# The start of a scan kernel: first rows by products of permuted rows, another layout in DRAM, scaling on other engines

## The chip, the cores and the metric

The kernel runs on one core of a Trainium2 chip, in one launch. Its time is device microseconds of that core; before the change the median of three runs is 4168.44 us (4168.14 to 4168.61).

## The reference, cut to what matters

Two layers follow each other on `x` of 32 images x 48 channels x 64 rows x 128 columns, float32. Each layer normalises (16 groups of 3 channels), then runs four scans, and adds the result to its input:

```python
def step(w, b):
    def f(carry, inp):
        nxt = inp + _conv1d(carry, w, b)      # 5 taps, 48 -> 48 channels
        return (nxt, nxt)
    return f
# rows downwards, rows upwards (same weights), columns to the right, columns to the left
x = x + _L0_conv_ref(_gn(x), ...)
x = x + _L1_conv_ref(_gn(x), ...)
```

In a scan step every row (or column) needs the one before it. Each layer has 63 + 63 row steps and 127 + 127 column steps.

## The kernel before, in words

**Tiling.** Images are taken in four groups of 8 (`GB`). The 128 partitions of a scan tile hold channels of 8 neighbouring positions of a line: 8 x 48 = 384 rows of channels make three tiles of 128 (`NG`), and ten `PIECES` say which channels of which position `e` (0 to 7) stand in which partitions of which tile. The free dimension holds 16 blocks x 8 images = 128 columns. One step (`step`, L889) is nine TensorE products of 128 columns, and three additions on DVE (`scalar_tensor_tensor`, L898), each of which adds bias and the next input row. In the profile one float32 product is two records.

**Order.** `PHASES` lists 12 phases: row scans for each group of images, column scans for each pair of groups, for each layer. `scans` gives the steps of a phase. Everything else stands in an agenda (`at(t, fn, ...)`), where t counts steps, and is issued when that step has been reached. `in_order` keeps every engine's instructions in the order in which they were written, so a waiting instruction holds all that stands behind it on its engine, and on SP's queue every transfer behind it. DMA completion is followed by eight semaphores that SP's and ACT's transfers take in turn: a transfer waits until the one eight places before it has landed.

**What has to happen before the first scan.** `x` in DRAM is ordered by image, channel, row and column; the scan wants its pieces. For the first group this is done in `first_group`, in two ways:

- All rows: `parts` are the images of the group in natural order, 128 partitions with 24 image rows each, 16 transfers of 768 KB. DVE takes their statistics (`InputStats.take`, L507, and `aggregate`, L510). `permute` (L659) turns one image row of all partitions into scan order with four copies of 128x256, on POOL or ACT. `put_out` writes it to the DRAM tensor `xin0`, 512 KB, on SP's queue; 24 such writes in all, in the order `order`, by `put_rows`. `move_rows` reads rows of the scan back from `xin0` in ten transfers (one for each piece) with runs of 128 bytes. Rows 8 to 11 need the first 16 writes, rows 12 to 15 all 24.
- Rows 0 to 7, in addition: `top` holds them with the channel as the partition (rows 0 to 3 in partitions 0 to 47, rows 4 to 7 in 64 to 111). `rows_by_product` (L1281) moves them into scan order by TensorE products with one-hot matrices (`selects`, from `shift`): ten products of 512 columns with 48 rows for each of the two sets, and a copy of each tile out of PSUM on ACT (L1288).

**Weights.** `place_kernel` (L1248) builds the first weight tile in the same way: 38 products of 6 to 390 columns with 48 rows, then copies on ACT (L1251, L1252).

**Scaling.** `scaling` makes scale and offset for each channel and image out of the statistics: products on PE (L385, L396), small operations on DVE, a square root on ACT (L428). Rows 0 to 3 are scaled by `scale_first` (15 instructions on DVE, L745, 9 on ACT, L747), rows 4 to 47 by `scale_rows` on ACT (L722, 24 instructions for each block of rows), rows 48 to 63 by `scale_at_once` on POOL (L733, one multiplication and one addition for a whole block, with scale and offset broadcast).

**Order on the engines.** PE: `place_kernel`, the products of the first set and one tile of the second, the products of `scaling`, two tiles of the second set, steps. SP: weights, `top`, `parts`, 18 writes, loads of rows 8 to 11, 6 writes, loads of rows 12 to 15, then of eight rows at a time. ACT: row copies of the products between permutes, the square root, scaling of rows 0 to 3, permutes, scaling of rows 4 on.

**Later uses of `xin0`.** In the first column phase `load_residual` reads the input of each image group again as columns (`x_by_col`, runs of 8 KB), 12 tiles of 1 MB for each group, to be added to the result (`add_residual`, L824).

Of the kernel before, what the change touches and what calls it, by code (L numbers as in the profile page):

```python
# [29 lines left out]
F32 = mybir.dt.float32  # L30
# [3 lines left out]
C = 48  # L34
# [85 lines left out]
def kernel(  # L120
# [62 lines left out]
    mask_in = wt["left"].rearrange("p i n -> p (i n)")[:, 5 * FULL : 5 * FULL + NG * C]  # L183
# [4 lines left out]
    def kept(name):  # L188
# [8 lines left out]
            dram.tile([E8 * NQ, C, UNIT], F32, tag=f"xin{g}", name=f"xin{g}")  # L197
            for g in range(NGRP)
# [36 lines left out]
    def x_by_col(t, e, j):  # L235


        return t[e * NQ + j]

# [421 lines left out]
    def put_out(g, r, perm):  # L661


        n = perm.shape[-1] // (W * GB)
        for i in range(n):
            at = slice(i * W * GB, (i + 1) * W * GB)
            dma(
                x_put(source[0][g], r + i),
                perm[:, at].rearrange("p (q n) -> p q n", q=NQ),
            )  # L670
# [8 lines left out]
    def move_rows(k, h0, h1, to_dram, q=None):  # L679
# [4 lines left out]
        for h in range(h0, h1, E8):  # L684
            end = min(h1, h + E8)
            for o in range(NG):
                for e, c0, c1, p0 in pieces(o):
                    here = view[p0 : p0 + c1 - c0, o, h % HALF : h % HALF + end - h]
                    if to_dram:
                        there = by_row(t, e, h, end, q)[c0:c1]  # L690
                    else:
                        there = x_by_row(t, e, h, end)[c0:c1]
# [21 lines left out]
    def scale_rows(k, h0, h1):  # L714
# [4 lines left out]
        for o in range(NG):  # L719
# [6 lines left out]
    def scale_at_once(k, h0, h1, eng):  # L726

        _, layer, g = PHASES[k]
        view = row_views(k)[h0 // HALF][:, :, h0 % HALF : h0 % HALF + h1 - h0]
        view = view.rearrange("p o h (k b) -> p o (h k) b", b=GB)  # L730
        for t, op in zip(coeffs[layer, g], (ALU.mult, ALU.add)):
            t = t.unsqueeze(2).to_broadcast([FULL, NG, (h1 - h0) * NK, GB])
            eng.tensor_tensor(view, view, t, op)  # L733

    def scale_first(k, h1, split):

        _, layer, g = PHASES[k]
        scale, offset = coeffs[layer, g]
        view = row_views(k)[0][:, :, 0:h1].rearrange("p o h (k b) -> p o b h k", b=GB)
        for b in range(GB):  # L740
            for o in range(NG):
                it = view[:, o, b]
                by, on = scale[:, o, b : b + 1], offset[:, o, b : b + 1]
                if b < split:
                    nc.vector.tensor_scalar(it, it, by, on, ALU.mult, ALU.add)  # L745
                else:
                    nc.scalar.activation(it, it, AF.Identity, bias=on, scale=by)  # L747
# [62 lines left out]
    def load_residual(k, j, i, nat):  # L810
# [6 lines left out]
        else:  # L817
            for e, c0, c1, p0 in pieces(o):
                dma(nat[p0 : p0 + c1 - c0], x_by_col(t, e, j)[c0:c1])
# [363 lines left out]
    def first_group():  # L1183
# [6 lines left out]
        whole = shift[:, 0 : 2 * FULL + start - C // 3 + ODD]  # L1190
        part = shift[:, whole.shape[-1] : whole.shape[-1] + FULL + ODD]
        SETS = ((0, C), (ODD, ODD + C))

        def selects(piece, s=0):
            e, c0, c1, o, p0 = piece
            t, at = (part, 0) if c0 and p0 else (whole, start - p0 + c0)
            p, q = SETS[s]
            return t[p:q, at + p : at + p + FULL]
# [3 lines left out]
        top = stage[:, 0:2].rearrange("p i n -> p (i n)").rearrange("p (b m) -> p b m", b=GB)  # L1202
        parts = [wide_nat(SLOT + i * SLOT, rows) for i in range(2)]
        stats = InputStats("x0", GB)
        n = W * GB

        kernel = slot[slots(0)[0]][0:C, 0 : TAPS * C + 6]
        zeros = slot[slots(0)[0]][0:C, 512 : 512 + NG * FULL + 6]

        def load_kernel():  # L1210
            nc.vector.memset(zeros, 0.0)
            for j in range(TAPS):
                d, si = divmod(TAPS - 1 - j, 2)
                to = kernel[:, j * C : (j + 1) * C]
                dma(to, w[SIDES[si], 0, DOWN, d, SIDES[0]], nc.scalar if j % 2 else nc.sync)
            aside(kernel[:, TAPS * C :], bias[0:C].rearrange("c l k -> c (l k)"))

        def make_ident():
            nc.vector.memset(shift[:, 0 : whole.shape[-1] + FULL + ODD], 0.0)
            for t, base in ((whole, start), (part, 2 * C - C // 3)):  # L1220
                nc.gpsimd.affine_select(
                    t,
                    t,
                    pattern=[[1, t.shape[-1]]],
                    compare_op=ALU.not_equal,
                    fill=1.0,
                    base=-base,
                    channel_multiplier=-1,
                )
            nc.gpsimd.memset(part[:, 0 : 2 * C], 0.0)  # L1230
            nc.gpsimd.memset(part[:, 2 * C - C // 3 + ODD : 2 * C + ODD], 0.0)

        def place_kernel():
            for i in range(NG):
                ps = ps_rows.tile([FULL, BN], F32, tag=f"rows{i}", name=f"rows{i}")
                todo = [(selects(PIECES[0]), zeros, slice(0, NG * FULL + 6))]
                for piece in PIECES:
                    e, c0, c1, o, p0 = piece
                    if o == i:
                        m = selects(piece)  # L1240
                        for run in WEIGHT_RUNS:
                            if run[0:4] == (c0, c1, i, p0):
                                _, _, _, _, at, to, n = run
                                todo.append((m, kernel[:, at : at + n], slice(to, to + n)))
                        tail = slice(NG * FULL, NG * FULL + 6)
                        todo.append((m, kernel[:, TAPS * C :], tail))
                for j, (lhs, rhs, to) in enumerate(todo):
                    nc.tensor.matmul(  # L1248
# [167 lines left out]
```

## Time and profile before

| | |
|---|---|
| median of three runs | 4168.44 us (4168.14 to 4168.61) |
| profiled execution | 4172.8 us, span 4171.0 us |
| mean granted TensorE clock | 0.99 |
| PE busy | 4073.2 us, 98% |
| DVE, ACT, POOL busy | 2135.8, 1287.2, 786.9 us |
| first scan step starts (timeline of PE) | 61.86 us |
| steps without a wait from (timeline of DVE) | 108.02 us |

The page is of one profiled execution. A busy share is an average over the whole span; the stretch that the change touches is the first 110 us or so, that is 2.6% of it, so it has to be read from the timelines of single engines. The granted clock is shown as 1.00 up to its first recorded change; the duration of a TensorE record says more there.

### The profile page before, as it was taken

What the parts mean: (1) busy time and instruction counts of PE and PEld (TensorE: products, weight loads), DVE (VectorE), ACT (ScalarE), POOL (GpSimd) and SP (SyncE); (2) the same over time, 40 slices, a digit from 0 to 9 for tenths busy, and PEclk for the clock granted to TensorE, in tenths of its full rate; (3) what the DMA queues carried; (4) which work ended last, traced back from release to release, by engine and by line L of the source; (5) the groups of instructions that cost most, each with busy time, mean ns of one, the idle gap of its engine ahead of it and who ended that gap; (6) DMA issues with size and microseconds to landing.
All of it is one profiled execution on the core that took longest, in us unless ns stands there. A gap on an engine that the chain in (4) does not pass through costs nothing. (4 is left out here: it accounts for less than half of the span.)

```text
span 4171.0 us, 90280 instructions
## 1 busy us (share of the span) xinstructions
PE 4073.2 (98%) x36724; PEld 4042.8 (97%) x36724; DVE 2135.8 (51%) x6501; ACT 1287.2 (31%) x2525; POOL 786.9 (19%) x737
## 2 busy tenths in 40 slices
PE   8999999999999999999999999999999999999994
PEld 6999989999999999999999999999999999999994
DVE  5454444456654454444447664444444444444444
ACT  6845000526974553000007863423000002200122
POOL 3530010434322010010014220000000005610353
PEclk9999999999999999999999999999999999999997
DMA  9987669669978999258409979959389019999699
GB/s 294 230 181 120 113 126 207 213 147 260 203 192 168 164 172 154 45 96 188 119 13 282 185 142 150 142 87 149 53 143 207 1 53 240 293 263 156 143 235 195
DMA packets 2206496, 680.57 MB, mean 163 GB/s; under 512 B 2008464, under 2 KB 2157184, under 8 KB 2179968
## 3 DMA queue, kind: packets, MB, share of 16 engines
q1 hardware_dynamic: 2062096, 582.09, 68.5%
q10 hardware_dynamic: 141424, 87.19, 8.7%
q8 instruction: 289, 4.73, 0.5%
q0 software_dynamic: 2560, 5.51, 0.5%
q14 instruction: 127, 1.04, 0.1%
HBM read 397.77 MB, written 295.14 MB: 166 GB/s over the span
## 5 line engine op out<-in xcount | busy, mean ns | idle before, releaser
L722 ACT ACTIVATE arena<-arena,offset,scale 128x256 f32<-128x256 f32 (+2 forms) x840 | 581.3, 791 | 346.9 <-DMA arena<-mid 179.9
L824 POOL TENSOR_TENSOR arena<-arena 128x2048 f32<-128x2048 f32 x80 | 362.6, 4547 | 1484.3 <-PE step_10l L889 462.8
L659 POOL COPY arena<-arena 128x256 f32<-128x256 f32 x332 | 196.6, 652 | 454.1 <-DMA arena<-in_x 406.9
L597 ACT ACTIVATE early<-arena 128x256 f32<-128x256 f32 x192 | 129.5, 675 | 446.0 <-POOL arena L824 439.9
L889 PE MATMUL step_00r<-arena,early 128*128 128x128 f32 x2286 | 252.5, 274 | 9.8 <-DMA arena<-arena 6.0
L889 PEld LDWEIGHTS step_00r<-arena,early 128*128 128x128 f32 x2286 | 251.8, 186 | 10.5 <-DVE arena L898 5.3
L889 PE MATMUL step_01r<-arena,early 128*128 128x128 f32 x2286 | 252.2, 274 | 7.0 <-DMA arena<-arena 5.9
L889 PEld LDWEIGHTS step_01r<-arena,early 128*128 128x128 f32 x2286 | 251.5, 186 | 7.6 <-issue 6.3
L889 PE MATMUL step_11r<-arena,early 128*128 128x128 f32 x2286 | 249.3, 272 | 0.0
L889 PE MATMUL step_00l<-arena,wleft 128*128 128x128 f32 x2286 | 249.2, 272 | 0.0
L889 PEld LDWEIGHTS step_11r<-arena,early 128*128 128x128 f32 x2286 | 248.7, 184 | 0.5 <-DVE arena L898 0.3
L889 PEld LDWEIGHTS step_00l<-arena,wleft 128*128 128x128 f32 x2286 | 248.7, 184 | 0.0
L889 PE MATMUL step_10l<-arena,wleft 128*128 128x128 f32 x2286 | 248.5, 272 | 0.0
L889 PE MATMUL step_11l<-arena,wleft 128*128 128x128 f32 x2286 | 248.5, 272 | 0.0
L889 PE MATMUL step_01l<-arena,wleft 128*128 128x128 f32 x2286 | 248.4, 272 | 0.0
L889 PE MATMUL step_10r<-arena,early 128*128 128x128 f32 x2286 | 248.4, 272 | 0.0
L889 PEld LDWEIGHTS step_10l<-arena,wleft 128*128 128x128 f32 x2286 | 248.4, 184 | 0.0
L889 PEld LDWEIGHTS step_11l<-arena,wleft 128*128 128x128 f32 x2286 | 248.4, 184 | 0.0
L889 PEld LDWEIGHTS step_01l<-arena,wleft 128*128 128x128 f32 x2286 | 248.4, 184 | 0.0
L889 PEld LDWEIGHTS step_10r<-arena,early 128*128 128x128 f32 x2286 | 248.4, 184 | 0.0
L282 ACT COPY early<-arena 128x1 f32<-128x1 f32 x2 | 0.4, 191 | 707.2 <-DVE arena L898 707.2
L846 ACT COPY arena<-arena 128x256 f32<-128x256 f32 x172 | 99.6, 657 | 363.0 <-POOL arena L824 272.8
(200 smaller groups left out, 7073.3 us busy)
## 6 DMA issues: line engine op xcount, KB each, us to landing
xin<-arena SPq DMA_DIRECT2D x91, 512.0 KB, 3.9
arena<-in_x SPq DMA_DIRECT2D x18, 2048.0 KB, 12.1
arena<-xin SPq DMA_DIRECT2D x96, 384.0 KB, 10.2
arena<-mid SPq DMA_DIRECT2D x384, 96.0 KB, 3.0
upb<-arena SPq DMA_DIRECT2D x192, 192.0 KB, 3.9
arena<-upb SPq DMA_DIRECT2D x96, 384.0 KB, 12.1
arena<-xin SPq DMA_DIRECT2D x180, 192.0 KB, 4.3
mid<-arena SPq DMA_DIRECT2D x32, 1024.0 KB, 11.2
```

Source lines behind the costliest of these rows:

```text
L282: fn(*args)
L597: nc.scalar.activation(junk[:, 0:n], view[:, b], AF.Identity, accum_out=self.sum[:, i, j : j + 1])
L659: copy(dst[:, r, q], src[:, r0 + r, q])
L722: nc.scalar.activation(args[0], args[0], AF.Identity, bias=args[2], scale=args[1])
L824: eng.tensor_tensor(unit, unit, nat, ALU.add)
L846: copy(by_w(perm)[:, a], src[:, a])
L889: nc.tensor.matmul(part(whole(ps[o])[0:m], -s), weights[:, i, at : at + m], part(src(i), s), start=seen[o] == 1, stop=seen[o] == left[o],)
```

## The change

- Rows 0 to 7: the image rows are loaded first, ahead of the weights, `top` gets 16 more channels in partitions 48 to 63 and 112 to 127, so that all 128 are filled; `permute` turns the four rows of `top` into `turned` (two on POOL, two on ACT), and the products read `turned` in runs of 32 elements. The selection matrices have 128 rows, one set for each half, with zeros in the other half.
- The products of rows 0 to 7 come ahead of `place_kernel`, which is split into its three tiles and stands between permutes; `kernel` and `zeros` are now 128 partitions, in `early`.
- `xin0` is laid out in natural order: channel, row, quarter, and within it 8 positions x 32. `put_out` writes 4 KB in one run for each partition instead of four of 1 KB; `move_rows` still reads runs of 128 bytes; `load_residual` reads runs of 1 KB instead of 8 KB for the first group.
- Rows 0 to 7 are scaled by `scale_at_once` on DVE, two rows at a time, rows 4 to 7 among the first steps. `scale_first` goes. Rows 8 to 39 are shared by `scale_shared`: tile 0 on ACT, tiles 1 and 2 on POOL. Rows 12 to 23 come in blocks of four rows, not in one of four and one of eight. The last permutes alternate between POOL and ACT.

```diff
         [
             dram.tile([E8 * NQ, C, UNIT], F32, tag=f"xin{g}", name=f"xin{g}")
+            if g
+            else dram.tile([C, H, NQ, LINE], F32, tag=f"xin{g}", name=f"xin{g}")
...
+    def natural_row(t, e, h0, h1):
+
+        return t.rearrange("c h q (e n) -> e c (h q) n", e=E8)[e, :, h0 * NQ : h1 * NQ]
+
+    def natural_put(t, r):
+
+        t = t.rearrange("c (a i) q n -> i (c a) (q n)", i=E8)[r % E8]
+        return t.rearrange("(p r) n -> r p n", r=PR // E8)[r // E8]
+
+    def natural_col(t, e, j):
+
+        return t.rearrange("c (a i) q n -> i q c a n", i=E8)[e, j]
 
...
+            one = perm[:, i * W * GB : (i + 1) * W * GB]
+            if g:
+                dma(x_put(source[0][g], r + i), one.rearrange("p (q n) -> p q n", q=NQ))
+            else:
+                dma(natural_put(source[0][g], r + i), one)
...
-                        there = x_by_row(t, e, h, end)[c0:c1]
+                        there = (x_by_row if g else natural_row)(t, e, h, end)[c0:c1]
...
+    def scale_rows(k, h0, h1, groups=range(NG)):
...
-        for o in range(NG):
+        for o in groups:
             for b in range(GB):
...
+    def scale_at_once(k, h0, h1, eng, o0=0):
 
         _, layer, g = PHASES[k]
...
+        view = row_views(k)[h0 // HALF][:, o0:, h0 % HALF : h0 % HALF + h1 - h0]
         view = view.rearrange("p o h (k b) -> p o (h k) b", b=GB)
         for t, op in zip(coeffs[layer, g], (ALU.mult, ALU.add)):
...
+            t = t[:, o0:].unsqueeze(2).to_broadcast([FULL, NG - o0, (h1 - h0) * NK, GB])
             eng.tensor_tensor(view, view, t, op)
-
...
-                dma(nat[p0 : p0 + c1 - c0], x_by_col(t, e, j)[c0:c1])
+                here = nat[p0 : p0 + c1 - c0]
+                if pair or half:
+                    dma(here, x_by_col(t, e, j)[c0:c1])
+                else:
+                    dma(by_line(here), natural_col(t, e, j)[c0:c1])
...
-        whole = shift[:, 0 : 2 * FULL + start - C // 3 + ODD]
-        part = shift[:, whole.shape[-1] : whole.shape[-1] + FULL + ODD]
+        span = 2 * FULL + start - C // 3 - ODD
         SETS = ((0, C), (ODD, ODD + C))
 
         def selects(piece, s=0):
             e, c0, c1, o, p0 = piece
-            t, at = (part, 0) if c0 and p0 else (whole, start - p0 + c0)
-            p, q = SETS[s]
-            return t[p:q, at + p : at + p + FULL]
+            at = s * (span + FULL)
+            at += span if c0 and p0 else start - p0 + c0
+            return shift[:, at : at + FULL]
 
...
+        top = wide_nat(3 * SLOT, four)
+        turned = stage[:, 2:4].rearrange("p i n -> p (i n)").rearrange("p (r n) -> p r n", n=n)
...
+        free = WEIGHTS + 2 * n
+        zeros = early[:, free : free + NG * FULL + 6]
+        free += NG * FULL + 6
+        kernel = early[:, free : free + TAPS * C + 6]
 
...
+                other = slice(ODD, FULL) if p0 == 0 else slice(0, ODD)
+                nc.gpsimd.memset(shift[other, at : at + span + FULL], 0.0)
+                nc.gpsimd.memset(part[:, 0 : 2 * C], 0.0)
...
         def rows_by_product(s, o):
-            src = top[SETS[s][0] : SETS[s][1]]
-            src = src.rearrange("p b (r k e) -> p e r k b", k=NK, e=E8)
             ps = ps_rows.tile([FULL, four * N], F32, tag=f"rows{o}", name=f"rows{o}_{s}")
+            src = turned.rearrange("p r (q e n) -> p e r q n", q=NQ, e=E8)
...
-                    ps.rearrange("p (r k b) -> p r k b", r=four, b=GB),
+                    ps.rearrange("p (r q n) -> p r q n", r=four, q=NQ),
...
+        def scale_shared(h0, h1):
+            scale_rows(0, h0, h1, range(1))
+            scale_at_once(0, h0, h1, pool, 1)
+
+        src = x[0:GB].rearrange("b c h w -> c b (h w)")
+        for s, (p0, p1) in enumerate(SETS):
+            here, queue = src[:, :, s * four * W : (s + 1) * four * W], (nc.sync, nc.scalar)[s]
+            dma(top[p0:p1], here, queue)
+            dma(top[p1 : p0 + ODD], here[0 : ODD - C], queue)
         load_kernel()
-        for s, (p0, p1) in enumerate(SETS):
-            src = x[0:GB].rearrange("b c h w -> c b (h w)")
-            dma(
-                top[p0:p1],
-                src[:, :, s * four * W : (s + 1) * four * W],
-                nc.scalar if s else nc.sync,
-            )
         for i in range(2):
             for b in range(GB):
                 dma(parts[i][:, b], flat(b)[:, i * rows * W : (i + 1) * rows * W])
...
         make_ident()
-        place_kernel()
+        for r in range(four):
+            permute(top, r, turned[:, r], ((pool, act)[r % 2],))
+        for o in range(NG):
+            rows_by_product(0, o)
         make_masks()
         for b in range(GB):
             stats.take(0, parts[0], b)
-        put_rows(pool, act, pool, act)
-        rows_by_product(0, 0)
-        put_rows(pool, act, pool, act)
-        rows_by_product(0, 1)
-        put_rows(pool, act, pool)
-        rows_by_product(0, 2)
-        put_rows(pool)
-        rows_by_product(1, 0)
+        for o in range(NG):
+            put_rows(pool, act)
+            rows_by_product(1, o)
+        for o in range(NG):
+            put_rows(pool, act)
+            place_kernel(o)
         for b in range(GB):
             stats.take(NBN // 2, parts[1], b)
             stats.aggregate(b)
         put_rows(act, pool)
         for _ in scaling("x0", 0, 0, stats, x_masks):
             pass
-        scale_first(0, 4, 5)
+        scale_at_once(0, 0, 2, nc.vector)
+        scale_at_once(0, 2, 4, nc.vector)
         put_rows(pool, act, pool, act)
-        rows_by_product(1, 1)
-        rows_by_product(1, 2)
         move_rows(0, 8, 12, False)
-        put_rows(pool, act, pool, pool, pool, pool)
-        move_rows(0, 12, 16, False)
-        scale_rows(0, 4, 8)
-        scale_rows(0, 8, 12)
-        scale_rows(0, 12, 16)
-        for h in range(16, 64, 8):
-            move_rows(0, h, h + 8, False)
+        put_rows(pool, act, pool, act, pool, act)
+        scale_shared(8, 12)
+        for h in (12, 16, 20, 24, 32, 40, 48, 56):
+            end = h + (four if h < 24 else E8)
+            move_rows(0, h, end, False)
             if h < 40:
-                scale_rows(0, h, h + 8)
+                scale_shared(h, end)
         take_in(1, 0, nats1[0])
 
     in_order(first_group)
+    at(starts[0] + 1, scale_at_once, 0, 4, 6, nc.vector)
+    at(starts[0] + 3, scale_at_once, 0, 6, 8, nc.vector)
     at(starts[0] + 10, scale_rows, 0, 40, 48)
     for j in range(1, 4):
         at(starts[0] + 22 + j, take_in, 1, 4 * j, nats1[j])
```

## The prediction

> **What bounds the kernel now.** I read the page first: TensorE is busy almost all of the span, and ahead of its first full slice there is an 8.
>
> ```profile
> span 4171.0 us, 90280 instructions
> PE 4073.2 (98%) x36724; PEld 4042.8 (97%) x36724; DVE 2135.8 (51%) x6501; ACT 1287.2 (31%) x2525; POOL 786.9 (19%) x737
> PE   8999999999999999999999999999999999999994
> ```
>
> So the scans are bound by TensorE, and this change can only win what the first 110 us lose. The profiled execution took 4172.8 us (span 4171.0, 1.8 outside it), 4.4 above the median 4168.44; I carry the difference found in the trace over to the median.
>
> Next the timeline of PE up to 130 us. Columns: start, duration, what, count (two records for one float32 product), idle before.
>
> ```profile
> 2.63 20.39 PE L1248 MATMUL rows<-arena,wleft 48*128 48x390 f32 x76 [2.63 <-POOL wleft L1221]
> 22.88 20.53 PE L1281 MATMUL rows<-arena,wleft 48*128 48x512 f32 x26
> 48.84 13.09 PE L1281 MATMUL rows<-arena,wleft 48*128 48x512 f32 x14
> 61.86 10.71 PE L889 MATMUL step_00d<-arena,early 128*128 128x128 f32 x74
> 74.60 8.16 PE L889 MATMUL step_00d<-arena,early 128*128 128x128 f32 x72 [2.03 <-DVE arena L898]
> 96.22 9.80 PE L889 MATMUL step_00d<-arena,early 128*128 128x128 f32 x72 [3.98 <-DVE arena L898]
> ```
>
> The first step starts at 61.86, held by the products of rows 0 to 7. Four steps (72 records) take 8.16 us at full rate, hence 0.113 us a record of 128 columns; the first 74 records took 10.71, 2.3 too many. The 512-column records of L1281 take 13.09/14 = 0.93 us; at the steps' rate they would take 0.45. So the preparation runs at half rate throughout, with 48 of 128 rows of the array in use, although PE is never idle in it.
>
> Then DVE's waits among the steps, and who ends them:
>
> ```profile
> 74.19 0.61 DVE L898 SCALAR_TENSOR_TENSOR arena<-step_00d,bd,arena 128x128 f32<-128x128 f32 x2 [2.28 <-ACT arena L722]
> 83.67 0.61 DVE L898 SCALAR_TENSOR_TENSOR arena<-step_00d,bd,arena 128x128 f32<-128x128 f32 x2 [1.48 <-ACT arena L722]
> 95.81 0.61 DVE L898 SCALAR_TENSOR_TENSOR arena<-step_00d,bd,arena 128x128 f32<-128x128 f32 x2 [4.24 <-ACT arena L722]
> 108.02 0.61 DVE L898 SCALAR_TENSOR_TENSOR arena<-step_00d,bd,arena 128x128 f32<-128x128 f32 x2 [2.57 <-DMA arena<-xin]
> ```
>
> These are rows 4, 8, 12 and 16. After 108.02 nothing stops PE until 577 us. So the number to predict is when row 16 can be added. Last, SP's queue and ACT, which deliver it:
>
> ```profile
> 63.73 6.06 SPq L271 DMA_DIRECT2D arena<-xin  x10
> 73.98 2.27 SPq L271 DMA_DIRECT2D xin<-early  x2
> 82.38 67.72 SPq L271 DMA_DIRECT2D arena<-xin  x68
> 64.65 18.93 ACT L722 ACTIVATE arena<-arena,offset,scale 128x64 f32<-128x64 f32 x48
> 86.22 24.27 ACT L722 ACTIVATE arena<-arena,offset,scale 128x64 f32<-128x64 f32 x53 [2.63 <-DMA arena<-xin]
> ```
>
> Rows 12 to 15 need all 24 `put_out` transfers on DRAM, so their loads start at 82.38 whatever PE does. Up to there the DMA engines are full (share 1.02 and 1.08 in the windows 23:43 and 49:61).
>
> **The change, part by part.**
>
> *Clock of the new products.* All products now use 128 rows. 20 products of 512 columns cost 20 x 1.86 = 37 us at half rate, 18 at full; `place_kernel` 20.4 or 10. No row of this trace shows selection products at 128 rows; the nearest are the steps: 128 rows, and after 61.86 they lose 2.3 us, so about 4.6 us at half rate, then full. I take full rate after 4.6 us. The Trainium skill (TensorE: Matmul & The Clock Gate, Part 1) says that about 3.4 us of sustained matmuls lift the clock, and names no number of rows; by it the products of before would have been fast too. The trace disagrees: 40 us of unbroken products stay at half rate. That leaves rows used, or something else in these products, as the reason, and the second is the first rival.
>
> *PE's order.* The image rows must land (about 12), then four `permute` calls, two on POOL and two on ACT, each 4 copies of 0.59: 4.7 us, to 16.5. First set 9 + 2.3 to 28, second set to 37, `place_kernel` to about 47. DVE's statistics (L507, from 12.67 to 44.5, unbroken) shift with the first part by about 1.5, to 46. So the scaling products wait for PE until 47, not 44.7; the scaling took 6.8 us (44.69 to 51.46), so the offsets come at 54.
>
> *Scaling of rows 0 to 7.* 15 + 9 instructions on DVE and ACT (7.4 us) become `scale_at_once` on DVE: 8 operations of 768 elements. L824 on DVE (2048 elements) takes 2.28 alone and 2.73 beside POOL's copies: 1.12 ns an element, so 0.86, plus up to 0.45. Rows 0 and 1: two, 2.6 us. First step at 57, 5 us earlier than 61.86. The last four operations stand among the steps; DVE has 0.7 to 1 us of idle between two steps, so each pair (1.7 to 2.6) delays PE by about 1. The skill's page SBUF — State Buffer speaks against this placing: a DVE operation with two SBUF inputs and a GpSimd one exclude each other. The 2.73 against 2.28 agrees in kind, 0.45 us each; at worst 8 x 0.45 = 3.6 us, but all of it before row 12.
>
> *What is late next.* From 57, steps reach row 4 at 67, row 8 at 75 and row 12 at 83. Row 12 isn't there, so the 5 us are off the path. Rows 12 to 15 come by the DMA stream:
> - The loads start at 0.80 instead of 2.18: -1.4. Two pads of 16 channels add 2 x 256 KB; at the 270 GB/s of the window 2:12 that is +1.9. They stand on both queues ahead of the weights, and semaphore lanes are shared by eight transfers, so `parts` now waits for the image rows to land: +1.2, an estimate between 0 and 3. Sum +1.7.
> - `put_out` writes 4 KB runs instead of four of 1 KB. The window 44:62 (1 KB runs) gives 379 GB/s, 13:37 (6 KB runs) 418, 696:708 (8 KB) 425. 512 KB: 1.38 against 1.25 us, 24 times: -3.1 (0 to -3.5).
> - SP's order is the same: 18 puts, 10 loads, 6 puts, loads. ACT's permutes end about 62 after its wait for the standard deviation at 51; no put waits for them, as the DMA needs put 17 at 64. Loads of rows 12 to 15 start at 82.38 + 1.7 - 3.1 = 81.0.
> - They keep runs of 128 B: 52 rows in 67.72 us, 1.30 a row. Four rows 5.2, landing 2.2: 88.4.
> - `scale_shared`: ACT 8 x 0.39, hidden beside POOL's two operations of 1024 elements. L733 (3072) takes 6.71, so 2 x 2.24 = 4.5. POOL has nothing else. Row 12 at 92.9 instead of 95.81.
> - PE then stood idle 10 us instead of 4. The 9.80 after a wait of 4 lost 1.6, the start 2.3; I take 2.3. Four steps 7.9 + 2.3: row 16 at 103.1. Rows 16 to 19 land at 93.6 and are scaled by 98: no wait. The next blocks are close: rows 24 to 31 land at about 109, two POOL operations of 2048 take 9, 118, and PE asks at 119.
>
> Sum: 103.1 against 108.02, -4.9; 4168.44 - 4.9 = 4163.5. Own range -9 to 0.
>
> *Natural order, later.* Residuals of group 0 (12 units) are read in 1 KB runs instead of 8 KB. In the window 852:878 these 48-partition loads run at 185 GB/s, in 1 KB runs 128-partition writes at 379, so run length isn't what limits them; I take nothing. But from 1000 to 1190 us the DMA share is 1.0, and PE waits 7.7 us for row data at 1193.06. 12 MB at 185 GB/s are 65 us; 10% either way gives or takes 6.5.
>
> **The rivals.**
> 1. *Half rate stays* (slower). If one-hot weights don't lift the clock, PE takes 37 + 20.4 from 16.5, to 74, then 6.8 and 2.6: first step at 83, row 12 not before 108. ACT's row copies and permutes wait between the products, so put 23 and the loads slide to about 98, row 12 to 110, row 16 to 119: +11, 4179.5. Against it: the steps' own rise. It decides from 12 us of delay on, which is how long PE may be late before row 12 asks.
> 2. *Full rate for the products, half for the weights* (products there have 6 to 390 columns). `place_kernel` ends at 57, put 15 is issued 3 us later, row 12 at 96, row 16 at 106: 4166.5.
> 3. *More than the sum*: the stream gains its 3.5, the wait at 1193 shrinks by up to 6.5: down to 4155, about 4158.
> 4. *Loads of natural order are slower*: the wait at 1193 grows by 15 or more: 4178.
>
> **How the numbers follow.** 0.2% is 8.3 us, about what a measurement can tell from no change. My case 0.38 and rival 2 0.12 lie within it: 0.50. Rival 3 0.30: faster. Rival 1 0.14 and rival 4 0.06: slower, 0.20. The range 4155 to 4180 takes in rival 3 and the middle of rivals 1 and 4; the likeliest case alone spans 4159 to 4168.
>
> **What would show it.** Right: 512-column records near 0.45 us after about 21 us; first step near 57; loads of rows 12 to 15 near 81 on SP; a longer idle ahead of row 12 than the 4.24 before, none at row 16. Wrong: records of 0.93 throughout; PE waiting at `place_kernel`'s end; loads of rows 12 before 78 or after 85; another length of the wait near 1190.

## The result, and the profile after

The median is 4177.6 us (12 runs, 4168.49 to 4184.83) against 4168.72 for the kernel before on the same chip: ratio 1.0021, interval 1.0012 to 1.0030. It is slower by 0.2%, about 9 us; 4163.5 was forecast. The profiled execution took 4171.1 us, 6.5 under its median, so it can't be compared by its total with the profile of before (4172.8, 4 above its median). I compare by place instead. First the head of the page:

```profile
span 4169.4 us, 90214 instructions
PE 4050.3 (97%) x36724; PEld 4033.1 (97%) x36724; DVE 2138.5 (51%) x6495; ACT 1251.3 (30%) x2440; POOL 828.6 (20%) x751
PE   5999999999999999999999999999999999999994
```

TensorE is busy 23 us less than before, since its preparation runs at full rate, and yet nothing is won: the first slice shows 5 instead of 8. Now the timeline of PE (start, duration, what, count, idle before; the views end at 130 and at 200 us, so the last two rows go on):

```profile
17.49 19.35 PE L1298 MATMUL rows<-arena,wleft 128*128 128x512 f32 x40 [17.49 <-POOL arena L674]
36.67 10.52 PE L1270 MATMUL rows<-early,wleft 128*128 128x390 f32 x76
59.46 5.57 PE L894 MATMUL step_00d<-arena,early 128*128 128x128 f32 x36 [6.11 <-DVE arena L748]
81.29 6.57 PE L894 MATMUL step_00d<-arena,early 128*128 128x128 f32 x36 [16.27 <-DVE arena L903]
88.03 42.23 PE L894 MATMUL step_00d<-arena,early 128*128 128x128 f32 x382 [0.16 <-DVE arena L903]
177.17 23.00 PE L894 MATMUL step_00d<-arena,early 128*128 128x128 f32 x192 [1.93 <-DVE arena L903]
```

The products and `place_kernel` end at 47.2, as forecast, and the first step starts 2.4 earlier than before. Then come two waits that were not forecast: 16.27 us after step 2, and 1.93 at 175, where the kernel before had none. DVE and POOL show their causes:

```profile
77.00 0.96 DVE L748 TENSOR_TENSOR arena<-arena,scale 128x768 f32<-128x768 f32 x1 [13.57 <-DMA xin<-arena]
78.00 2.98 DVE L748 TENSOR_TENSOR arena<-arena,offset 128x768 f32<-128x768 f32 x1
176.76 0.87 DVE L903 SCALAR_TENSOR_TENSOR arena<-step_00d,bd,arena 128x128 f32<-128x128 f32 x3 [3.11 <-POOL arena L748]
```

```profile
77.05 3.11 POOL L748 TENSOR_TENSOR arena<-arena,scale 128x1024 f32<-128x1024 f32 x1 [11.66 <-DMA xin<-arena]
163.25 6.69 POOL L748 TENSOR_TENSOR arena<-arena,scale 128x3072 f32<-128x3072 f32 x1 [28.28 <-DMA arena<-xin]
170.02 6.71 POOL L748 TENSOR_TENSOR arena<-arena,offset 128x3072 f32<-128x3072 f32 x1
```

The scaling of rows 4 and 5 waits for a `put_out`, though no put touches these rows. Rows 48 to 55 (3072 elements on POOL) are ready at 176.7, and DVE, which adds row 48, has waited 3.11 us. Before the change, the same scaling started 10.6 us earlier:

```profile
152.65 6.69 POOL L733 TENSOR_TENSOR arena<-arena,scale 128x3072 f32<-128x3072 f32 x1 [90.33 <-DMA arena<-xin]
```

The row loads on SP are late, and SP's waits from 120 to 170 us (below the rows of its queue: us in total, times, longest) say for whom:

```profile
12.57 18.03 SPq L286 DMA_DIRECT2D arena<-in_x  x16
66.57 5.59 SPq L286 DMA_DIRECT2D arena<-xin  x10
82.30 81.90 SPq L286 DMA_DIRECT2D arena<-xin  x80
```

```profile
SPq L286 <- POOL arena L748: 8.9, 1, 8.9
```

`parts` is issued from 12.57, not 2.65. Loads of rows 12 on start at 82.30, against 82.38 before, and take 81.90 us. Before, all of these loads had landed by 155.0; now by 167.5. Once, for 8.9 us, SP stands behind POOL.

**A ledger by rows.** As PE has no wait of over 0.35 us between row 51 and 570 us in any run, the moment when DVE adds row 51 sums up the opening. The table gives the start of that addition and of earlier ones, from the DVE timelines; the last column is the median less row 51. (Row 16's first addition starts at 105.10 before and at 111.24 after the change; the 108.02 of the prediction are its second and third.)

| run | row 17 | row 25 | row 51 | median | before, same chip | ratio, interval | rest |
|---|---|---|---|---|---|---|---|
| before | 109.59 | 125.39 | 176.75 | 4168.44 | | | 3991.7 |
| before_again | 109.70 | 125.50 | 176.85 | 4168.27 | 4169.14 | 1.0003 (0.9994 to 1.0012) | 3991.4 |
| after | 113.16 | 128.96 | 184.19 | 4177.60 | 4168.72 | 1.0021 (1.0012 to 1.0030) | 3993.4 |
| after_again | 113.19 | 128.99 | 184.64 | 4178.72 | 4171.57 | 1.0018 (1.0009 to 1.0027) | 3994.1 |
| put_pieces | 107.74 | 126.28 | 185.97 | 4185.98 | 4169.70 | 1.0035 (1.0022 to 1.0048) | 4000.0 |
| put_pieces_again | 107.12 | 125.56 | 184.69 | 4179.53 | 4169.14 | 1.0023 (1.0014 to 1.0033) | 3994.8 |
| pool_by_tile | 111.80 | 127.60 | 178.95 | 4175.85 | 4169.70 | 1.0012 (1.0004 to 1.0021) | 3996.9 |
| rows32_by_tile | 112.64 | 128.44 | 179.79 | 4176.11 | 4167.96 | 1.0018 (1.0010 to 1.0027) | 3996.3 |
| tiles_one_by_one | 107.50 | 123.77 | 175.12 | 4170.64 | 4171.57 | 1.0003 (0.9993 to 1.0013) | 3995.5 |
| old_layout | 111.66 | 127.61 | 186.18 | 4183.00 | 4171.57 | 1.0026 (1.0017 to 1.0035) | 3996.8 |
| before_natural | 108.00 | 125.42 | 176.77 | 4173.48 | 4171.57 | 1.0004 (0.9995 to 1.0012) | 3996.7 |
| tiles_weights_first | 104.80 | 122.36 | 173.72 | 4166.94 | 4169.70 | 0.9992 (0.9983 to 1.0001) | 3993.2 |
| pieces_pool_weights | 106.39 | 122.19 | 173.54 | 4168.60 | 4169.70 | 0.9997 (0.9988 to 1.0006) | 3995.1 |
| rows96_no_pad | 103.48 | 119.46 | 170.81 | 4166.61 | 4167.96 | 0.9994 (0.9986 to 1.0002) | 3995.8 |
| rows96_again | 103.70 | 120.01 | 171.36 | 4166.40 | 4169.14 | 0.9992 (0.9984 to 1.0001) | 3995.0 |
| rows64 (one run) | 116.21 | 132.01 | 185.59 | 4183.68 | 4167.96 | | 3998.1 |

The changed kernel loses 7.4 to 7.9 us by row 51: 3.6 by row 17, the rest at rows 48 to 50. That is as much as the 7 to 9 of the medians.

### The profile page after: what moved, and what is told of

Its sections match the earlier page's. It is cut to its first block, busy times and chain, and to the rows that moved or that the text cites. A ratio compares the mean times of both kernels' runs of the same rounds, so it can differ in the third digit from the quotient of the medians.

```text
span 4169.4 us, 90214 instructions
## 1 busy us (share of the span) xinstructions
PE 4050.3 (97%) x36724; PEld 4033.1 (97%) x36724; DVE 2138.5 (51%) x6495; ACT 1251.3 (30%) x2440; POOL 828.6 (20%) x751
## 5 line engine op out<-in xcount | busy, mean ns | idle before, releaser
L737 ACT ACTIVATE arena<-arena,offset,scale 128x256 f32<-128x256 f32 (+2 forms) x744 | 538.1, 817 | 386.8 <-DMA arena<-mid 147.7
## 6 DMA issues: line engine op xcount, KB each, us to landing
arena<-upb SPq DMA_DIRECT2D x96, 384.0 KB, 12.3
```

The lines of the kernel that those rows point to most:

```text
L737: nc.scalar.activation(args[0], args[0], AF.Identity, bias=args[2], scale=args[1])
```

## The experiments

Theory one: an operation that spans several tiles (rows 4 and 5 of all three, `128x3x256`, one tile 32 rows apart from the next) is made to wait for every transfer that uses the rows in between, and holds later transfers itself. Theory two: the natural order in DRAM makes loads or later residuals slower.

**The changed kernel again.** No edit.

> The changed kernel once more, for a second profile and more times: its first profile (4171.1 us) is near the low end of its 12 runs (4168.5 to 4184.8), so most of the 9 us to the kernel before may lie in waits that the first profile does not show. Both theories: median 4175 to 4180. Theory one (the wait of the spanning DVE operation): the 13.6 us wait of DVE ahead of row 4 is there again, row 16 is added at 111 +- 1. Theory two (natural order in DRAM): row 16 the same, but the later waits of PE (near 175, 584, 1188 and 1857 us), 19.7 us in sum in the first profile against 27.8 before the change, come out larger here, by up to 10 us, if the profiled execution is a slower one.

Row 51 at 184.64, DVE's wait 13.30, median 4178.72: as theory one says, but theory two gave the same for row 16 and the median, so this run does not decide between them. PE's waits of over 0.35 us after 100 us were 24.6 instead of 19.7 us in sum (a wait at 607 us of 3.86 instead of 0.47): the rest of the kernel varies by some us from one execution to the next.

**One operation for each tile.**

```diff
         for t, op in zip(coeffs[layer, g], (ALU.mult, ALU.add)):
-            t = t[:, o0:].unsqueeze(2).to_broadcast([FULL, NG - o0, (h1 - h0) * NK, GB])
-            eng.tensor_tensor(view, view, t, op)
+            for o in range(o0, NG):
+                it = t[:, o].unsqueeze(1).to_broadcast([FULL, (h1 - h0) * NK, GB])
+                eng.tensor_tensor(view[:, o - o0], view[:, o - o0], it, op)
```

> The changed kernel, with scale_at_once as one operation for each of the tiles instead of one across two or three tiles. Theory one (an operation that spans tiles waits for every transfer that uses the rows between): the first operation of rows 4 and 5 starts by 66 with less than 2 us of idle ahead of it, instead of 77.00 after 13.57; row 8 is added near 84 instead of 95.53, row 12 near 96 (its rows are ready on GpSimd at 95), row 16 near 104 instead of 111.24; the median falls by 7 from that of the changed kernel, to about 4170. Theory two (the time is lost by the natural order in DRAM, in the later waits): the trace up to row 16 changes as just said, but the median stays within 3 of the changed kernel's, about 4176.

DVE and PE of this run:

```profile
65.36 1.08 DVE L749 TENSOR_TENSOR arena<-arena,scale 128x256 f32<-128x256 f32 x3
96.52 25.88 PE L895 MATMUL step_00d<-arena,early 128*128 128x128 f32 x216 [4.53 <-DMA arena<-xin]
```

The operations of rows 4 and 5 start at 65.36 without a wait, PE has no wait of over 0.35 us from 96.52 to 570, the last row loads are issued by 157.2, and the median falls by 8.1 to 4170.64 (4178.72 on the same chip). The spanning operations cost what the change lost. Which of them, this run can't say.

**The layout of before in the changed kernel; natural order in the kernel before.** In the first, `xin0`, its puts, row loads and residual loads are as before the change; in the second these four are the only change.

> The changed kernel, with the DRAM tensor of the first group laid out as before the change (each put again four runs of 1 KB, residuals again in runs of 8 KB). Theory one: puts take 1.38 instead of 1.25 us, 24 of them 3.1 us; rows 12 to 15 land 3 us later, row 16 is added near 114; median 4178 to 4181. Theory two: the later waits shrink and lose their spread (before: 9 us in 12 runs, after: 16), median 4170 or below.

> The kernel before, with the natural order in DRAM alone. Theory one: puts 1.25 instead of 1.38 us, loads of rows 12 to 15 start at 79.5 instead of 82.4, row 16 is added near 105 instead of 108; median 4166, 0 to 3 below the kernel before. Theory two: slower than the kernel before by 5 to 9, median 4174 to 4177, with a wider spread and larger waits of PE near 580 and 1190.

SP and ACT of before_natural:

```profile
78.36 73.41 SPq L286 DMA_DIRECT2D arena<-xin  x70
64.89 60.41 ACT L737 ACTIVATE arena<-arena,offset,scale 128x64 f32<-128x64 f32 x135
```

Natural order alone brings the loads of rows 12 to 15 forward by 4.0 us (82.38 to 78.36). Row 16 gains 4.1, and by row 19 all of it is gone: ACT, which does all the scaling there, works without a break from 64.89 to 125.30 and is late next. The median is 1.9 higher, and the interval reaches from 2 below to 5 above: theory two's loss of 5 to 9 is not seen, and neither is theory one's gain of 0 to 3. In old_layout loads of rows 12 start at 86.32, 4.0 later, row 51 comes at 186.18 and the median rises by 4.3 to 4183.00. Theory one said 4178 to 4181, theory two 4170 or below, so theory two falls, and theory one has the direction and too small a size. One thing was not expected by either: old_layout has no wait ahead of rows 4 and 5, although its operation spans the tiles as well, and row 16 comes at 109.74, not near 114.

**The puts described otherwise.** What differs for DVE between the two layouts is how the put is written on the SBUF side, one run of 1024 or four of 256. So this run changes the description alone:

```diff
-                dma(natural_put(source[0][g], r + i), one)
+                there = natural_put(source[0][g], r + i)
+                there = there.rearrange("p (q n) -> p q n", q=NQ)
+                dma(there, one.rearrange("p (q n) -> p q n", q=NQ))
```

> The changed kernel, with one line of put_out: the transfer's two sides are written as four runs of 256 each that follow each other (the same 4 KB for each partition, natural order in DRAM). Instructions, their order and the transfer itself stay; only the waits that the compiler derives differ: the DVE operations of rows 0 to 7 span three tiles as before. Theory one (the 13.6 us wait is a dependence that the compiler sees between the spanning DVE operation and a put of one run, and no data need it): the operation of rows 4 and 5 starts by 65, row 12 is added near 95 (GpSimd is done with its rows at 95.0), row 17 near 107.5 instead of 113.2; GpSimd's spanning operations stay, so row 48 still waits, and rows 48 to 50 lose 2 to 4 as they do in the changed kernel; median 5 to 6 below the changed kernel, near 4173. Rival (rows 4 to 7 wait for data that they need, or for DVE itself): the wait stays over 10 us and the median within 2 of 4178.7.

PE (the view ends at 200 us) and POOL:

```profile
57.37 5.76 PE L896 MATMUL step_00d<-arena,early 128*128 128x128 f32 x36 [4.90 <-ACT arena L674]
124.81 49.08 PE L896 MATMUL step_00d<-arena,early 128*128 128x128 f32 x430 [2.17 <-DVE arena L905]
177.98 22.23 PE L896 MATMUL step_00d<-arena,early 128*128 128x128 f32 x176 [4.08 <-DVE arena L905]
164.06 6.71 POOL L750 TENSOR_TENSOR arena<-arena,scale 128x3072 f32<-128x3072 f32 x1 [28.74 <-DMA arena<-xin]
```

The wait of 13.6 us is gone with instructions, order and bytes unchanged, so it came from the compiler's view of the overlap, not from data. Why it sees an overlap with one run of 1024 and none with four of 256 was not settled. Row 17 comes at 107.74 as expected. But the median did not fall by 5; it rose by 7. All that was won is lost again: row 25 waits for POOL (2.17), row 48 for POOL (4.08; SP again stands 8.9 us behind POOL), since POOL starts rows 48 to 55 at 164.06 whatever PE has won. So the largest gap of PE, 16.27 us, was worth nothing by itself. The Trainium skill (Perfetto Trace Analysis, Optimization Strategy) advises to find the gaps of the contended engine and to start what blocks them sooner; here that, done at the largest gap alone, gave no gain.

> The run with puts in four runs again, as its median (4186.0, of 6 undisturbed runs) lies 7 above the changed kernel's, while its row 51 is only 1.3 later. If the start of the kernel accounts for the time, row 51 is at 186.0 again and the median is 8 to 12 above the kernel before, near 4180. If taking away DVE's wait costs more later on, the median is again 14 or more above it.

The second time: row 51 at 184.69, median 4179.53, 10.4 above the kernel before. The 4186 seems a high draw of what follows row 51 (rest 4000.0, here 3994.8); that taking away DVE's wait gains nothing holds in both.

**GpSimd by tile; its rows 32 to 39 alone by tile.** The loop of tiles_one_by_one, for POOL only (`if eng is nc.gpsimd:`), and for one block of rows only:

```diff
+            if o0 and h0 == HALF:
+                for o in range(o0, NG):
+                    it = t[:, o].unsqueeze(1).to_broadcast([FULL, (h1 - h0) * NK, GB])
+                    eng.tensor_tensor(view[:, o - o0], view[:, o - o0], it, op)
+                continue
```

DVE's operations span as in the changed kernel.

> The changed kernel, with GpSimd's scaling by tile, DVE's as changed. Theory one: DVE's wait of 13.6 us ahead of row 4 stays and row 17 stays at 113.2; SP's wait of 8.9 us for GpSimd at the loads of rows 40 to 47 goes, the last row loads are issued by 157 instead of 164.4, GpSimd begins with rows 48 to 55 near 141 instead of 163.7, and PE doesn't wait at row 48: row 51 is 3.6 behind the kernel before instead of 7.4 to 7.9; median 4 below the changed kernel, 4174 to 4175. Rival (that wait is contention with DVE or late loads, not the spanning): row 48 waits 2 us or more as in the changed kernel.

> The changed kernel, with GpSimd's scaling of rows 32 to 39 alone by tile (two multiplications and two additions of 1024 elements instead of one each of 2048); all other scaling as changed, DVE's spanning operations too. Theory (one spanning operation holds one transfer of rows 40 to 47 on SP's queue, and with it all row loads behind it, which costs the wait at row 48): SP's wait of 8.9 us for GpSimd goes, the last row loads are issued by 156, GpSimd begins with rows 48 to 55 near 154 instead of 163.7, PE doesn't wait at row 48, row 51 is 3.6 behind the kernel before instead of 7.4 to 7.9 (DVE's wait of 13 us stays, row 17 at 113); median near 4175, as by tile on GpSimd altogether (4175.9). Rival (it takes all of GpSimd's operations, or the load rate of the natural order): row 48 still waits 2 us or more, median within 2 of 4178.7.

POOL of rows32_by_tile; then the window of 124 to 136 us, first of the changed kernel, then of rows32_by_tile (PE, PEld, DVE, ACT, POOL busy, clock, DMA share, GB/s):

```profile
122.99 4.68 POOL L750 TENSOR_TENSOR arena<-arena,scale 128x1024 f32<-128x1024 f32 x2
154.93 6.71 POOL L753 TENSOR_TENSOR arena<-arena,scale 128x3072 f32<-128x3072 f32 x1 [22.62 <-DMA arena<-xin]
```

```profile
124.00:136.00 12.00, 12.00 (x111) 12.00 (x111) 5.92 (x19) 4.22 (x8) 9.07 (x2) 1.00 0.33 52
```

```profile
124.00:136.00 12.00, 12.00 (x112) 12.00 (x111) 5.75 (x18) 7.46 (x15) 8.32 (x4) 1.00 0.98 149
```

Splitting one multiplication and one addition in two takes SP's wait away. In the changed kernel the DMA engines moved 52 GB/s in that stretch, because the first load of rows 40 to 47 of tile 1 (issued at 135.00, 9.8 after the one before it) stood behind the scaling of rows 32 to 39 of tiles 1 and 2; between these rows it lies in memory. In this run they moved 149, the loads were issued by 155.1, POOL began 8.3 us earlier and row 48 did not wait. Row 51 is at 179.79, 4.4 to 4.9 earlier, as expected; with all of POOL by tile, 178.95. Their medians, 4176.1 and 4175.9, are 8.2 and 6.2 above the kernel before, more than the 3.0 and 2.2 of row 51. The rest column says the same: these two have 3996 to 3997. In the whole time the ratios, 1.0018 and 1.0012, can't be told from the changed kernel's 1.0021 and 1.0018: what POOL's wait alone costs is shown at row 51, and not at the end.

So with both spans the loss at row 51 is 7.4 to 7.9; without DVE's, 7.9 and 9.2; without POOL's, 2.2 and 3.0; without both, -1.6. Each hides the other in part: at row 51 POOL's alone keeps all of the loss, DVE's alone 2.2 to 3.0. In the whole time only the run without both is clearly lower.

**The start of the stream.** Weights ahead of the image rows, as before the change, with scaling by tile on both engines; then the same with the puts in four runs and DVE's spanning operations.

```diff
+        load_kernel()
         for s, (p0, p1) in enumerate(SETS):
...
             dma(top[p1 : p0 + ODD], here[0 : ODD - C], queue)
-        load_kernel()
```

> Scaling by tile on DVE and GpSimd, and the weights issued ahead of the image rows as before the change. Theory (the stream of puts and loads sets row 12, and the image rows ahead of the weights hold parts back by lanes: parts from 12.57 instead of 2.65): parts are issued from about 3, loads of rows 12 to 15 start 3 to 4 earlier than the 84.0 of the run by tile, row 17 is added near 104 (107.5 by tile), median 3 to 4 below the run by tile, 4167. Rival (the DMA engines are full from 2 us on whichever comes first): the image rows land later, the permutes and products slide, and the loads of rows 12 to 15 start within 1.5 of 84.0; median within 2 of 4170.6.

> Puts described in four runs, DVE's scaling across tiles, GpSimd's by tile, weights ahead of the image rows. Theory: as in the run by tile with weights first, but DVE's first scaling takes 8 operations of 768 instead of 24 of 256, so the first step comes 2 to 3 earlier; this is off the path, and row 17 and the median are the same as there within 2: row 17 near 104, median 4167. If the first step counted, the median would be 2 to 3 lower than in that run.

`parts` is issued from 2.6 us, and loads of rows 12 to 15 start at 82.11, 1.9 earlier than by tile, not 3 to 4. Row 17 comes at 104.80 and row 51 at 173.72, 1.4 earlier than by tile. In the second run row 1 is added 2.7 earlier (61.15 instead of 63.90), row 17 1.6 later (106.39; 104 was expected), and row 51 is the same within 0.2: the first step is off the path.

**96 rows without pads.**

```diff
-        SETS = ((0, C), (ODD, ODD + C))
+        SETS = ((0, C), (C, 2 * C))
+        USED = 2 * C
...
-            return shift[:, at : at + FULL]
+            return shift[0:USED, at : at + FULL]
...
-            dma(top[p1 : p0 + ODD], here[0 : ODD - C], queue)
```

> As the run with puts in four runs, GpSimd by tile and weights first, but the image rows stand in partitions 0 to 47 and 48 to 95, without the two transfers of 16 more channels, and the products and weights use 96 rows of the array. Theory (the pads and the slow image rows, 211 GB/s from 2 to 12 us, hold the stream of puts): loads of rows 12 to 15 start 1.5 to 2.5 earlier than 82.5, at 80 to 81; row 17 at 104 to 105 instead of 106.4; median 2 below that run, near 4166. On the clock: if it goes by rows used, 96 could lie on either side; at half rate the products take 37 us and the weights 20, PE is done with them at 74, and the first step comes near 83, median over 4180; at full rate 512-column records near 0.45 as with 128. I expect full rate.

> The version with 96 rows and no pads again, against the kernel before: row 51 5.9 ahead of it in the trace, median 1.4 below in the first comparison, interval 0.9986 to 1.0002. If the 5.9 us hold to the end, median 4 to 6 below the kernel before; if the rest of the kernel takes more when it starts earlier, 1 to 2 below as before.

SP, first of pieces_pool_weights, then of this run:

```profile
31.97 14.92 SPq L286 DMA_DIRECT2D xin<-arena  x9
82.50 73.75 SPq L286 DMA_DIRECT2D arena<-xin  x80
```

```profile
28.76 14.88 SPq L286 DMA_DIRECT2D xin<-arena  x9
79.35 73.88 SPq L286 DMA_DIRECT2D arena<-xin  x80
```

Without the two pads, 512 KB, the stream is 3.2 us earlier. Row 51 is 5.9 and 5.4 ahead of the kernel before, but the medians are only 1.4 and 2.7 below it, and both intervals hold 1. With tiles_weights_first (2.8 below) these are the lowest versions found; none is a proven gain.

In the two profiles of this version the clock is lifted 5.25 and 4.70 us after the first product. In the second profile it does not hold: `place_kernel` takes 11.79 us instead of 10.53, and the granted clock falls to 0.50 at 45.9, while PE is still busy without a break. First the row of `place_kernel`, then the window that follows the fall, with the clock ahead of the DMA share and the GB/s:

```profile
36.90 11.79 PE L1286 MATMUL rows<-early,wleft 96*128 96x390 f32 x76
45.90:48.70 2.80, 2.80 (x15) 2.80 (x15) 0.00 (x0) 0.51 (x1) 1.22 (x3) 0.50 1.03 416
```

**64 rows.** The first set's products read partitions 0 to 63, the second's 64 to 127; `place_kernel` reads 0 to 63.

```diff
-            return shift[:, at : at + FULL]
+            return shift[s * ODD : s * ODD + ODD, at : at + FULL]
...
-                    src[:, piece[0]],
+                    src[s * ODD : s * ODD + ODD, piece[0]],
```

> The changed kernel, with the products of rows 0 to 7 and of the weights on 64 rows of the array instead of 128. One look at the clock: records of 512 columns near 0.93 throughout, as with 48 rows before the change (40 us without a change of clock), if 64 rows are too few; near 0.45 after some 4 us if 64 suffice. I expect half rate: the first step then comes near 83 and the time is about 10 us over the changed kernel.

Windows of this run (PE, PEld, DVE, ACT, POOL busy, granted clock, DMA share, GB/s; up to the first recorded change, here at 35.1, the clock is shown as 1.00 in any case):

```profile
17.00:31.00 14.00, 13.54 (x16) 5.43 (x17) 13.89 (x23) 1.22 (x3) 4.14 (x17) 1.00 1.01 419
31.00:35.50 4.50, 4.50 (x11) 2.24 (x10) 4.46 (x9) 0.57 (x2) 4.50 (x8) 1.00 1.02 418
35.50:45.80 10.30, 10.30 (x51) 7.01 (x50) 10.13 (x20) 10.30 (x21) 8.88 (x16) 0.98 1.01 416
45.80:55.00 9.20, 9.20 (x41) 8.57 (x41) 3.05 (x7) 5.31 (x13) 6.74 (x12) 0.50 1.03 417
```

The changed kernel at full rate starts 37 records in 15.5 us; here 16 in 14, so half rate. Between 31.28 and 34.9 the records start in pairs (31.28 and 31.28, 32.13 and 32.30, 32.98 and 33.15): a product of the second set, in rows 64 to 127, beside one of the first, in rows 0 to 63. At 35.1 the clock is lifted, after 3.8 us of such pairs, and at 45.3 it falls to 0.50, though PE is never idle between; with 128 rows `place_kernel` ran at full rate to its end. So products of 64 rows alone did not lift the clock in 13.8 us, nor hold it through `place_kernel`. The first step comes at 64.67, not near 83, and the time of this one run is 5 to 6 above the changed kernel's medians, not 10.

**The kernel before again.**

> The kernel before once more, for a second profile: one says that row 51 is added at 176.75 and that 3994 us follow in the profiled execution, 3990 to 3993 in the medians. If the start of the kernel is the same in each execution, row 51 is within 0.5 of 176.75 here, and only what follows varies, 3985 to 3999; median within 2 of 4169.

Row 51 at 176.85, 0.10 from the first profile, and PE's waits of over 0.35 us after 100 us 21.6 instead of 27.8 in sum. The opening is nearly the same in each execution (two profiles of the changed kernel differ by 0.45 at row 51, of put_pieces by 1.3); what follows varies by more.

## Why the prediction was wrong

- *Clock of the new products*: right. The clock rose at 21.4 us; 512-column records come every 0.43 us, `place_kernel` took 10.52 (10 forecast). Rivals 1 and 2 fell with it. One reading was too strong: in the kernel before, PE did wait in its preparation, 1.27 and 0.96 us between 43 and 49 us; the 40 us ahead of that are unbroken, so the argument stands.
- *PE's order*: end of `place_kernel` 47.2 (47), statistics 48.98 (46), offsets 55.46 (54), first step 59.46 (57). Of the 2.5 us, 1.4 come with the late statistics, and 1.12 are a wait of the first scaling operation, which spans the tiles too, for a put (until 56.58). They are off the path, as said and as pieces_pool_weights shows.
- *Scaling of rows 0 to 7*: the first four operations took 1.27 to 1.45 (0.86 to 1.31 forecast). What the pairs among the steps cost is the first failed step, below.
- *What is late next*, the stream: natural order gave 4.0 (3.1 forecast; before_natural). The start cost 4.4, puts from 32.80 instead of 28.41 (1.7 forecast). Of that the pads are 3.2 (1.9 forecast). The rate of 270 GB/s behind the 1.9 was misread: the window 2:12 of the kernel before shows 247, and here the image rows come in at 212. Issuing the image rows ahead of the weights costs 1.1 at the puts (32.78 by tile, 31.66 with weights first) and 1.9 at the loads (84.02, 82.11; 1.2 forecast). Loads at 82.30 instead of 81.0.
- **The steps that failed** are two, and in both I priced an operation across tiles by its elements and not by what it waits for and holds. The first is in the sum: "each pair delays PE by about 1". The first operation of the second half (rows 4 and 5) waited 13.57 us for a put, PE stood for 16.27, and row 16, forecast for 103.1, began at 111.24. With one operation a tile it began at 105.58, with puts in four runs at 105.82 and 105.20. The second is where the sum ended: "After 108.02 nothing stops PE until 577 us. So the number to predict is when row 16 can be added." That is true of the kernel before. I followed POOL up to rows 24 to 31 and took no look at rows 32 on, where `scale_shared` meets loads on SP's queue. There the new operation held a load for 8.9 us and every load behind it, and row 48 became late. rows32_by_tile shows this by splitting one pair of operations. At row 51 the forecast was 4.9 ahead of the kernel before, and the changed kernel is 7.4 to 7.9 behind. Of these 12.3 to 12.8 us, 9.1 to 9.5 go when no operation spans tiles (1.6 ahead then). The 3.3 that are left fit the mis-sized start of the stream: the loads of rows 12 to 15 start at 84.02 in that run, 3.0 later than forecast.
- *Rivals*: the slower side was right, by a mechanism that I did not list. That 4177.6 lies between 4155 and 4180 is luck: the slow end stood for rivals 1 and 4, and neither came. Rival 3 fell. Rival 4 (natural order makes loads slower) fell with before_natural and old_layout: in before_natural the 70 row loads are issued over 73.41 instead of 69.94 us, but end at 151.8 instead of 152.3. The wait near 1190, which was to grow by 15 or more, is 6.8 us there and 4.6 in the changed kernel, 7.4 before.
- *Natural order, later*: stays open within some us. The rest column is 3991 to 3992 for the kernel before (up to 3995 with its medians in the other comparisons) and 3993 to 3997 for nearly all others, of either layout. Why it is some us higher, and why an opening that is 5.9 us shorter gives 1.4 to 2.7, was not settled; one profile of each can't sample waits that vary by 5 us.

## What to carry to other kernels

An operation with a stride across tiles can be given waits for transfers that only use the memory between the tiles, and can hold such transfers itself. Whether it is depends on how the transfer is described (here one run or four). Before tiles are joined in one instruction, ask which transfers use the memory in between, and afterwards read the waits of both. When work is moved to another engine, follow its whole list of operations against the loads behind it, not only to the place where the old kernel was last late. And take a gap for a gain only if what is late next is known: taking away the 16 us gap alone gave nothing at row 51, taking away an unnoticed wait of 8.9 us on a queue gave 4 to 5.

## What the runs showed of the hardware

**How many rows of the array are in use matters to the clock.** The products were unbroken from the start in all of these runs. With 128 rows (ten profiles) the clock was lifted 2.95 to 6.09 us after the first product, 3.9 in the changed kernel, and held to the end of `place_kernel`. With 96 rows it was lifted after 5.25 and 4.70 us, within that spread, and in one of the two profiles it fell again during `place_kernel`. With 64 rows it was not lifted in 13.8 us, until the other 64 were used beside them, and it fell 10 us after that. With 48 rows, in the kernel before, it was not lifted in 40 us. Only the run with 64 rows changes nothing but the rows that the products use; the kernel before also reads its rows with another stride. Both falls came during `place_kernel`, with products of 6 to 390 columns, so whether their width has a part in it is open. The Trainium skill (TensorE: Matmul & The Clock Gate, Part 1) gives about 3.4 us of sustained matmuls, as a time alone, and names no number of rows. The runs with 128 and 96 rows agree with it nearly; those with 64 and 48 do not, and there the measurement decides.

**A DVE operation with two inputs in SBUF and a GpSimd one exclude each other.** Look again at 77 us in the DVE and POOL lines above: DVE's 0.96 at 77.00 is followed by 2.98 at 78.00, while POOL's 3.11 from 77.05 runs to 80.16. The same operation takes 0.96 alone (at 86.75), POOL's 2.37. The second DVE operation ends 0.8 after POOL's, about its own length, and POOL's took 0.7 longer than alone: as if each had waited for the other's whole instruction. The Trainium skill (SBUF — State Buffer, SBUF: two separate sides) says just that, an exclusive lock for the whole instruction. The prediction had 0.45 for each from the rows of before; here one operation lost 2.0 beside a POOL operation of 2.4 us.
